# A four-layer network in three stages: 24 tile buffers of the second stage handed out by one plan

## The chip, the cores and the metric

The kernel runs on one core of a Trainium2 chip. The metric is the device time of one execution in microseconds (us). The times shown are medians of the runs; a profile is of one further execution, whose own time stands beside its span. Five engines work side by side, each in the order of its own queue: PE (TensorE, matmuls), DVE (VectorE), ACT (ScalarE), POOL (GpSimd) and SP (SyncE, which here only issues transfers). They wait for each other through semaphores.

## The reference

The input x is 8192 samples of 8 x 16 x 16 numbers in float32. Four layers follow, each a normalisation over groups of channels, a transformation, and a sum with its input:

```python
    # _gn: mean and variance over each of 4 groups of 2 channels, per sample
    # layer 0: three small tensor factors ("tensor train") and a bias
    x = x + _L0_conv_ref(_gn(x), L0_conv_core0, L0_conv_core1, L0_conv_core2, L0_conv_bias)
    # layer 1: 3x3 convolution, batch normalisation over all samples, gamma, beta, relu
    x = x + _L1_conv_ref(_gn(x), L1_conv_lin_w, L1_conv_lin_b, L1_conv_gamma, L1_conv_beta)
    # layer 2: 3x3 convolution of x quantised to -127..127 by the largest |x| of ALL samples
    x = x + _L2_conv_ref(_gn(x), L2_conv_weight, L2_conv_bias)
    # layer 3: 3x3 convolution with binarised weights, edge padding
    x = x + _L3_conv_ref(_gn(x), L3_conv_weight, L3_conv_bias)
```

Two of the steps need all samples before any can go on: the batch normalisation of layer 1 (its mean and variance) and the largest absolute value in layer 2. They cut the kernel into three stages.

## The kernel before, in words

The 8192 samples are 64 tiles (`NT = 64`) of 128 samples; one tile is 128 partitions x 2048 float32, 1 MB (`F = 2048`). A tile does not stay on the core from stage to stage: it is written to memory and read again, except where a buffer is kept for it.

**First stage.** For each tile layer 0 and the convolution of layer 1. It leaves two tensors a tile: `x1_d[t]` (x after layer 0) and `y_d[t]` (the convolution's result, not yet normalised). The last four tiles (`STAY = 4`) are not written: their x stands in the four `xs` buffers, their y in `ys` and `bs` (`y_stay`). The first stage also uses `xls`, two 1 MB buffers into which the split halves ("limbs") of a normalised tile are fetched; they are read by the matmuls of `expand`, and no more after the last of these.

**Between.** A small pool `bn` is opened after the first stage's pools are closed. In it the batch normalisation becomes a scale `bn_a` and a shift `bn_b` (lines 713 to 725). It is closed, and the pool `more` is opened with two tile buffers `xk`.

**Second stage** (from line 743). It takes the tiles in `order2`: the four that stayed first, then the others. For tile i:

- `relu2` (ACT) makes relu(bn_a y + bn_b) in place; `add2` (POOL) and `addv2` (DVE) add it to x, in the shares of the table `SPLIT`;
- `square2` (ACT) and `sums2` (64 matmuls) make the sums for the next normalisation, `stats2` (DVE reduction), `means2` (ACT), `sigma2` (DVE) and `power2` (POOL) turn them into mean and 1/sigma, `wide2` and `spread2` lay these out in PSUM;
- `centre2` subtracts the mean from x (DVE, a share `POOL2` of some tiles on POOL);
- `range2` takes maxima of the absolute value over w, `top2` (once for four tiles) scales and reduces them: these give the largest |x| of all;
- `store2` writes the centred x to `x2_d`, except for 15 tiles (`KEEP`) whose buffers are kept for the third stage.

Each of these steps has a time in a made-up clock of 6 units a tile: `when(op, i) = 6 i + PHASE2[op] + SHIFT2[...]`, the last for the final tiles only. All steps of all tiles, loads and stores too, are sorted by these times and written out in that order. The times thus fix only the order in each engine's queue, not when anything runs. SP's queue holds all loads and stores of this stage, so a transfer whose buffer is not free, or whose tile is not yet centred, holds those behind it.

The buffers before: x uses a ring of 15 (`x_slots`: the four `xs`, two `ex`, the halves of the two `us`, two `xk`, `ys`, `ys`, `bs`), y a ring of 8 (`y_slots`: `bs`, two `sq`, `xh`, four `yk`). x of tile i is loaded some 8 tiles before its use, y some 7; the last six tiles (`LATE = 6`) get theirs through `late2`, one load after each addition, into buffers of y that are just free. Tiles 43 to 57 are the 15 kept ones; 0 to 42 and 58 to 63 are stored. Nine loads (into `ex`, `us`, `sq`, `xh`) are written in the first stage's last steps. Two buffers (tag `sq2`) hold the squares.

**Third stage** (from line 908). It quantises by the largest |x|, and runs layers 2 and 3, first on the kept tiles, then on the others, which `load3` reads back into the same 15 buffers. Its first instruction on a tile is the DVE product `v`.

Nearly all engine instructions pass through one helper, so that they carry its line 43 in the profile; transfers carry the line of their own: 125 `load2`, 867 `late2`, 848 `store2`, 927 `load3`.

Of the kernel before, what the change touches and what calls it, by code (L numbers as in the profile page):

```python
# [8 lines left out]
F32 = mybir.dt.float32  # L9
F32R = mybir.dt.float32r  # L10
# [8 lines left out]
P = 128  # L19
C, H, W = 8, 16, 16  # L20
CH = C * H
F = P * W
G = 4
R = 8
NQ = 4
# [4 lines left out]
KEEP = 15  # L30


class InOrder:
# [5 lines left out]
    def __getattr__(self, name):  # L39
        op = getattr(self.engine, name)  # L40

        def call(*args, **kwargs):
# [13 lines left out]
TURN = 6.0  # L56
PHASE2 = {"relu": 0.0, "add": 0.3, "sums": 12.6, "rows": 18.9, "spr": 19.2, "sq": 7.5, "red": 13.8, "cp": 14.1, "cen": 20.4,
          "store": 20.7, "sig": 15.0, "pow": 15.3, "rng": 21.6, "top": 21.9, "addv": 0.31}
SHIFT2 = {-5: {"top": 9.4, "relu": -3, "sq": -1.3},
          -4: {"top": 18.3, "rng": 10.2, "cen": 1.4, "store": 11.7},  # L60
          -3: {"store": 4.0, "sums": -0.3, "cen": 3, "top": 33.8, "rng": 6.4, "sq": -4.0},
          -2: {"sums": -3.7, "spr": 1.0, "store": 8.4, "relu": -8.6, "rng": 12.1, "sq": -3.0, "top": 46.0, "red": -2.6},
          -1: {"cp": 0.1, "addv": 2.0, "red": 0.3, "pow": 1.3, "top": 60.5, "rng": 58.5, "store": 39.9, "spr": 10.6,
            "cen": 16.3, "relu": -4.3, "sq": -1.0}}

SPLIT = {0: 0.5, 1: 0.5, 2: 0.5, 3: 0.5, -2: 0.25, -1: 0.75, -3: 0.25}
POOL2 = {-4: 0.5, -3: 0.5, -2: 0.5, -1: 0.5, -5: 0.25}
SHARE = 24
# [8 lines left out]
def tile_net(ctx: ExitStack, tc: tile.TileContext, xb, xt_in, pack0, pack1, pack2, out):  # L77
    nc = tc.nc
    NT = xt_in.shape[0]
# [5 lines left out]
    x1_d = [dram.tile([P, F], F32, name=f"x1_d{t}", tag=f"x1_d{t}") for t in range(NT)]  # L85
    y_d = [dram.tile([P, F], F32, name=f"y_d{t}", tag=f"y_d{t}") for t in range(NT)]
    limb_d = [dram.tile([2, QS, 4 * BANK], F32, name=f"limb_d{k}", tag=f"limb_d{k}") for k in range(4)]
    x2_d = [dram.tile([P, F], F32, name=f"x2_d{t}", tag=f"x2_d{t}") for t in range(NT)]
# [13 lines left out]
    us = [hold.tile([P, 2 * F], F32, name=f"u{k}") for k in range(2)]  # L102

    STAY = 4
    order2 = list(range(NT - STAY, NT)) + list(range(NT - STAY))
    y_stay = [ys[NT % 2], ys[(NT - 1) % 2], bs[NT % 2], bs[(NT - 1) % 2]]
    y_of = dict(zip(order2, y_stay))

    x_slots = ([xs[t % 4] for t in order2[:STAY]] + ex + [u[:, h * F:(h + 1) * F] for u in us for h in range(2)] + y_stay[:3])
    y_slots = [y_stay[3]] + sqs + [xh]  # L110
    T2 = [dict() for _ in range(NT)]

    LATE = 6 if NT >= KEEP + STAY + 3 else 0
    stays = order2[max(0, NT - KEEP - LATE):NT - LATE]
    order = [*stays, *(t for t in range(NT) if t not in stays)]
    place = {t: i for i, t in enumerate(order)}

    def load2(i, what="yx"):
        for k in what:
            if k == "x":  # L120
                T2[i]["x"] = x_slots[i % KEEP]
            else:
                T2[i]["y"] = y_stay[i] if i < STAY else y_slots[(i - STAY + 1) % len(y_slots)]
            if i >= STAY:
                nc.sync.dma_start(T2[i][k], (x1_d if k == "x" else y_d)[order2[i]])


    first = ExitStack()
    const1 = first.enter_context(tc.tile_pool(name="const1", bufs=1))
    w0 = load_pack(pack0, PACK0, const1.tile(list(pack0.shape), F32, name="w0"))  # L130
# [211 lines left out]
    with first as s:  # L342
# [5 lines left out]

        T = [dict() for _ in range(NT)]

# [8 lines left out]

        xls = [const1.tile([P, F], F32R, name=f"xl{k}") for k in range(2)]  # L360

# [255 lines left out]
        for n in range(NT * NQ):  # L617
# [57 lines left out]
            if quarter_of(n, LAG):  # L675
                conv1(*quarter_of(n, LAG))
            for i, k in {NT * NQ - 6: [(0, "x"), (1, "x")], NT * NQ - 2: [(0, "y"), (2, "x"), (1, "y"), (3, "x")]}.get(n, []):
                load2(STAY + i, k)

        t = NT - 1  # L680
        seen = max(1, NT - 2)
        shift, nmean, part, last = bnw[:, 0:1], bnw[:, 1:2], bnw[:, 2:4], bnw[:, 4:6]
        dve.tensor_reduce(shift, bnst[:, 0:seen, 0], AX.X, ALU.add)
        load2(STAY + 4, "x")
        load2(STAY + 5, "x")
        conv1_output(t - 1, 1)
# [3 lines left out]
        quarter_apply(t, 2)  # L690
        load2(STAY + 2, "y")
        conv1_direct(t, 1)
# [49 lines left out]

    more = ctx.enter_context(tc.tile_pool(name="more", bufs=1))
    small = ctx.enter_context(tc.tile_pool(name="small", bufs=4))
    kept = {}
    with tc.tile_pool(name="p2", bufs=2) as p2, tc.tile_pool(name="ps2", bufs=2, space=PSUM) as ps2:
        T = T2
        x_slots[STAY + 6:STAY + 6] = [more.tile([P, F], F32, name=f"xk{k}") for k in range(2)]
        y_slots += [p2.tile([P, F], F32, name=f"yk{k}", bufs=1) for k in range(4)]
        psc = ps2.tile([P, 96], F32, name="psc2", tag="psc2", bufs=1)  # L750
# [39 lines left out]
        def square2(i):  # L790
            T[i]["sq"] = p2.tile([P, F], F32, name=f"sq2_{i}", tag="sq2")
            act.activation(T[i]["sq"], T[i]["x"], AF.Square)
# [51 lines left out]
        def store2(i):  # L844
            if NT - KEEP - LATE <= i < NT - LATE:
                kept[order2[i]] = T[i]["x"]
            else:
                nc.sync.dma_start(x2_d[order2[i]], T[i]["x"])

# [13 lines left out]

        def late2(n):
            k, j = "yx"[n % 2], NT - LATE + n // 2
            T2[j][k] = T[NT - LATE - AHEAD2 - 1 + n]["y"]
            nc.sync.dma_start(T2[j][k], (x1_d if k == "x" else y_d)[order2[j]])

        def when(op, i, more=0.0):
            return TURN * i + PHASE2[op] + SHIFT2.get(i - NT, {}).get(op, 0) + more  # L870

        AHEAD2, TURNX = len(y_slots) - 1, KEEP - 3
        for i in range(STAY):
            load2(i)
        for i, k in [(3, "y"), (6, "x"), (4, "y"), (7, "x"), (5, "y"), (6, "y")]:
            load2(STAY + i, k)
        OPS2 = {"relu": relu2, "add": add2, "addv": addv2, "sums": sums2, "rows": wide2, "spr": spread2, "sq": square2,
                "red": stats2, "cp": means2, "cen": centre2, "store": store2, "sig": sigma2, "pow": power2, "rng": range2,
                "top": top2}
        todo2 = [(when(op, i), OPS2[op], (i,)) for i in range(NT) for op in OPS2]  # L880
        todo2 += [(when("relu", i - AHEAD2, -.2), load2, (i, "y")) for i in range(STAY + AHEAD2, NT - LATE)]
        todo2 += [(when("add", i - TURNX, .6) if i < KEEP else when("relu", i - 8, -.1), load2, (i, "x"))
                  for i in range(TURNX, NT - LATE)]
        todo2 += [(when("add", NT - LATE - AHEAD2 - 1 + n, .6), late2, (n,)) for n in range(2 * LATE)]
        todo2.append((when("relu", NT // 2, -.3), operands3, ()))
        for _, f, args in sorted(todo2, key=lambda e: e[0]):
# [21 lines left out]
    with ExitStack() as s:  # L908
# [3 lines left out]
        T, T3 = [dict() for _ in range(NT)], {}  # L912
        AHEAD = min(NT, KEEP - 8)
        diag3 = diagonal("d")
# [6 lines left out]
        def load3(i):  # L921
            t = order[i]
            if t in kept:
                T[i]["x"] = kept[t]
                return
            T[i]["x"] = x_slots[(NT - KEEP - LATE + i) % KEEP]
            nc.sync.dma_start(T[i]["x"], x2_d[t])

# [243 lines left out]
```

## Time and profile before

| | us |
|---|---|
| median of 3 runs | 3795.26 (3795.01 to 3795.76) |
| the profiled execution: its time | 3795.71 |
| its span, first to last instruction | 3793.9 |
| second stage begins: first relu | 2625.94 |
| second stage ends: last maximum over a tile's values (starts 3046.16, takes 0.28) | 3046.44 |
| third stage begins: first `v` on DVE | 3051.20 |

The chain that ended last runs 79% on PE, 10% on DVE and 7% over transfers. Whole-span shares are averages over three different stages: PE is busy 94% of the span, DVE 87%, POOL 79%, ACT 67%; in the second stage PE is busy only half the time (13.74 of 20 us in the window from 2640), while the 16 transfer engines are full. The transfer queue of SP moves 688.03 MB in the whole kernel. A row of the timeline reads: start in us, duration, engine, line, operation, what is written and read (buffer numbers left out, so `yk` is any of the four), the shapes, how many, and in brackets the idle time before and what ended it. A row of SyncE gives the issue of a transfer, not its length.

### The profile page before, as it was taken

How to read it: one execution, taken by the hardware profiler on the slowest of the kernel's cores; microseconds unless marked ns; L12 is line 12 of the kernel's file. 1: busy time of each engine (PE TensorE's matmuls, PEld its weight loads, DVE VectorE, ACT ScalarE, POOL GpSimd, SP SyncE). 2: the span in 40 equal slices, each digit the busy share in tenths (PEclk: the TensorE clock that was granted, in tenths of full speed). 3: DMA queues.
4: the chain of work that ended last, by engine and by line, in shares of the span. 5: the costliest groups of instructions: out<-in, count | busy, mean ns of one | idle time of the engine just before them, and what ended most of it. 6: DMA issues, size and time to landing. Idle time of an engine off the chain costs nothing.

```text
span 3793.9 us, 63755 instructions
## 1 busy us (share of the span) xinstructions
PE 3568.5 (94%) x21896; PEld 2295.5 (61%) x21960; DVE 3317.6 (87%) x5963; ACT 2543.2 (67%) x2807; POOL 2990.9 (79%) x3102
## 2 busy tenths in 40 slices
PE   8999999999999999999999999998655569999999
PEld 4666666666666666666666666665544446666666
DVE  8888888888888888888888888887987888889887
ACT  5666666666666666666666666665765668888886
POOL 4877777777777778778777777775987869999998
PEclk9999999999999999999999999998776889999999
DMA  6787887887887887878878878865999824444432
GB/s 225 258 272 253 260 269 255 261 269 253 262 269 255 260 266 252 268 258 256 270 253 261 272 250 264 270 205 228 424 425 426 333 101 189 189 189 189 190 133 112
DMA packets 210276, 957.45 MB, mean 252 GB/s; under 512 B 44832, under 2 KB 45088, under 8 KB 109984
## 3 DMA queue, kind: packets, MB, share of 16 engines
q1 hardware_dynamic: 173232, 688.03, 48.7%
q0 software_dynamic: 36288, 264.26, 23.5%
q8 instruction: 175, 2.87, 0.3%
q14 instruction: 149, 1.22, 0.1%
q10 hardware_dynamic: 432, 1.08, 0.1%
HBM read 576.75 MB, written 376.44 MB: 251 GB/s over the span
## 4 chain that ended last, share of the span: by engine, by line
PE 79%; DVE 10%; DMA 7%; POOL 2%; issue 1%; ACT 1%; SPq 0%; DVEq 0%; POOLq 0%; ACTq 0%
PE po L43 45%; PE pu L43 12%; PE pf L43 6%; PE pm L43 6%; DVE v L43 3%; PE pc L43 3%; PE pq L43 3%; PE s L43 2%; DMA sq<-y_d 2%; DMA x_d<-u 1%; DMA ys<-x_d 1%; PE ps_a L43 1%; DVE top L43 1%; DVE xs L43 1%; DVE ys L43 1%
## 5 line engine op out<-in xcount | busy, mean ns | idle before, releaser
L43 PE MATMUL po<-u,core 128*128 128x512 f32 (+1 forms) x4112 | 1844.6, 591 | 0.6 <-DVE xs L43 0.6
L43 ACT COPY u<-pu 128x2048 f32<-128x2048 f32 x512 | 956.5, 1868 | 515.9 <-PE pu L43 515.9
L43 PEld LDWEIGHTS po<-u,core 128*128 128x128 f32 x4112 | 744.9, 190 | 737.4 <-issue 735.4
L43 PE MATMUL pu<-core2r,xl 128*128 128x256 f32 x4032 | 678.5, 310 | 4.8 <-ACT u L43 3.5
L43 PEld LDWEIGHTS pu<-core2r,xl 128*128 128x128 f32 x4032 | 527.9, 189 | 128.1 <-issue 123.1
L43 POOL TENSOR_TENSOR bs<-bs,xh 128x512 fp32r<-128x512 f32 (+1 forms) x253 | 325.8, 1288 | 202.1 <-ACT xh L43 202.1
L43 POOL TENSOR_TENSOR v<-e 128x128 f32<-128x128 f32 x750 | 397.3, 541 | 0.0
L43 DVE TENSOR_TENSOR xs<-po,xs 128x512 f32<-128x512 f32 x256 | 176.9, 691 | 220.2 <-PE po L43 220.2
L43 ACT ACTIVATE m<-pm,b 128x128 f32<-128x128 f32 x250 | 92.0, 368 | 396.7 <-PE pm L43 396.7
L43 PEld LDWEIGHTS pm<-v,fast 128*128 128x128 f32 x2000 | 262.5, 191 | 119.7 <-issue 106.4
L43 POOL TENSOR_TENSOR e<-x1n,x 128x512 f32<-128x512 f32 x250 | 306.0, 1224 | 26.4 <-ACT x L43 19.3
L43 DVE TENSOR_TENSOR bs<-bs,stat 128x1024 f32<-128x1024 f32 x252 | 290.5, 1214 | 2.1
L43 POOL TENSOR_TENSOR xs<-xs,w 128x2048 f32<-128x2048 f32 x64 | 291.5, 4555 | 0.6 <-DMA xs<-in_xt 0.6
L43 PE MATMUL pm<-v,fast 128*128 128x128 f32 x2000 | 263.5, 275 | 0.0
L43 ACT ACTIVATE x<-x1n 128x512 f32<-128x512 f32 x500 | 247.0, 545 | 7.6 <-DVE x1n L43 7.6
L43 PE MATMUL pf<-hi,sign 128*128 128x512 f32 x768 | 229.2, 434 | 0.0
L43 POOL DMA_DIRECT2D xl<-limb_d x252 | 150.0, 595 | 94.8 <-ACT x L43 33.8
L43 PE MATMUL pf<-lo,sign 128*128 128x512 f32 x768 | 217.6, 419 | 2.7 <-ACT lo L43 2.7
L43 POOL TENSOR_TENSOR v<-r 128x128 f32<-128x128 f32 x500 | 215.5, 447 | 0.0
L43 POOL TENSOR_TENSOR mvb<-mvb,mhalf 128x4 f32<-128x4 f32 x64 | 66.3, 1036 | 162.7 <-DVE mvb L43 142.7
L43 PE MATMUL pq<-q,band 128*128 128x480 bf16 (+1 forms) x704 | 186.7, 385 | 7.7 <-ACT q L43 4.1
L43 PE MATMUL gb<-ident,wide 128*128 128x128 f32 x128 | 42.3, 424 | 157.4 <-ACT wide L43 156.4
(337 smaller groups left out, 7303.3 us busy)
## 6 DMA issues: line engine op xcount, KB each, us to landing
xl<-limb_d POOLq DMA_DIRECT2D x252, 1024.0 KB, 7.4
x_d<-xs SPq DMA_DIRECT2D x72, 1024.0 KB, 8.4
xs<-in_xt SPq DMA_DIRECT2D x64, 1024.0 KB, 7.6
bs<-in_xb SPq DMA_DIRECT2D x63, 1024.0 KB, 5.8
limb_d<-xh SPq DMA_DIRECT2D x1008, 64.0 KB, 4.2
limb_d<-bs SPq DMA_DIRECT2D x1008, 64.0 KB, 5.2
y_d<-ys SPq DMA_DIRECT2D x60, 1024.0 KB, 8.1
yk<-y_d SPq DMA_DIRECT2D x30, 1024.0 KB, 19.6
```

Source lines behind the costliest of these rows:

```text
L43: return self.tc.keep_in_program_order(op(*args, **kwargs))
```

## The change

- `plan2` takes the place of the two rings and of `late2`. It walks through all wanted loads in order of time (a y is wanted 8.22 tiles before its relu, an x 7.54 tiles before its addition: `AHEAD2`) and gives each the buffer of one common set of 24 that its table of free times has free first. A buffer of y is taken to be free half a tile (`FREE2`) after its addition, one of x 0.8 tiles after its store. `BEGIN2` holds when the 16 loose buffers first come free.
- The stores of tiles 0 to 40 are written at 5.39 tiles behind the tile's start (`BEHIND2`), where before they came at 20.7 units, 3.45 tiles. Of the last 23 tiles 15 are kept; eight (`LATE = 8`) are stored as soon as they are centred, and the plan picks which: 51, 52, 56 and 58 to 62. Kept are 41 to 50, 53, 54, 55, 57 and 63.
- The buffers: one `sq2` fewer, one `yk` more (five). The two `xk` of the pool `more` now lie where the `xls` lay, since these have got a pool of their own, `limbs1`, opened ahead of all others of the first stage. The plan's first loads after `xh` go to these two.
- The nine loads in the first stage fill the same nine buffers, with y and x of tiles 4 to 7 and y of tile 8.
- New tables `SHIFT2`, `SPLIT` and `POOL2` for the last tiles: among others the addition of tile 62 is wholly DVE's, of 57 a quarter, of 60 and 63 a half; of the centring POOL does a half for tiles 59, 60 and 63, a quarter for 57, 61 and 62.
- The third stage takes its buffers from the plan (`x3`).

```diff
-SPLIT = {0: 0.5, 1: 0.5, 2: 0.5, 3: 0.5, -2: 0.25, -1: 0.75, -3: 0.25}
-POOL2 = {-4: 0.5, -3: 0.5, -2: 0.5, -1: 0.5, -5: 0.25}
+SPLIT = {0: 0.5, 1: 0.5, 2: 0.5, 3: 0.5, -2: 1, -1: 0.5, -7: 0.25, -4: 0.5}
+POOL2 = {-4: 0.5, -3: 0.25, -2: 0.25, -1: 0.5, -7: 0.25, -5: 0.5}
+AHEAD2 = {"y": 8.22, "x": 7.54}
+BEHIND2, LATE = 5.39, 8
+FREE2 = {"y": 0.5, "x": 0.8}
+BEGIN2 = {"ex0": -83.5, "ex1": -83, "sq0": -82.5, "sq1": -52, "u0": -30, "u1": -29.3, "u2": -21.8, "u3": -21.4,
+          "xh": -16.3, "xl0": -16.2, "xl1": -16.1, "yk0": -1.5, "yk1": -1.5, "yk2": -1.5, "yk3": -1.5, "yk4": -1.5}
...
+    LOOSE = {"y_3", "sq0", "sq1", "xh", *(f"yk{k}" for k in range(5))}
+    def plan2():
+        centred = [when("cen", i) + .05 for i in range(NT)]
+        stores = {i: max(centred[i], TURN * (i + BEHIND2)) for i in range(NT - KEEP - LATE)}
+        free = [(t, n) for n, t in BEGIN2.items()]
...
+        for want, k, i in wanted:
+            k, now = "yx"[k], max(want, last)
+            free.sort()
+            pick = free[0]
+            if k == "x" and i not in stores:
+                firm = [e for e in free if e[1] not in LOOSE]
+                if late < LATE and (not firm or firm[0][0] > now and pick[0] < firm[0][0]):
+                    late, stores[i] = late + 1, centred[i]
+                else:
+                    pick = firm[0]
+            elif k == "y" and i > NT - KEEP - LATE - 8:
+                pick = ([e for e in free if e[1].startswith("yk") and e[0] <= now] + [pick])[0]
+            free.remove(pick)
+            last = max(now, pick[0] + .05, last + .001)
+            T2[i][k] = pick[1]
+            loads.append((last, i, k))
...
     first = ExitStack()
+    limbs1 = first.enter_context(tc.tile_pool(name="limbs1", bufs=1))
     const1 = first.enter_context(tc.tile_pool(name="const1", bufs=1))
...
-        xls = [const1.tile([P, F], F32R, name=f"xl{k}") for k in range(2)]
+        xls = [limbs1.tile([P, F], F32R, name=f"xl{k}") for k in range(2)]
...
-            for i, k in {NT * NQ - 6: [(0, "x"), (1, "x")], NT * NQ - 2: [(0, "y"), (2, "x"), (1, "y"), (3, "x")]}.get(n, []):
-                load2(STAY + i, k)
+            early2(*{NT * NQ - 6: ("ex0", "ex1", "sq0"), NT * NQ - 2: ("sq1", "u0", "u1")}.get(n, ()))
...
     more = ctx.enter_context(tc.tile_pool(name="more", bufs=1))
+    tiles.update({f"xl{k}": more.tile([P, F], F32, name=f"xk{k}") for k in range(2)})
...
-        x_slots[STAY + 6:STAY + 6] = [more.tile([P, F], F32, name=f"xk{k}") for k in range(2)]
-        y_slots += [p2.tile([P, F], F32, name=f"yk{k}", bufs=1) for k in range(4)]
+        tiles.update({f"yk{k}": p2.tile([P, F], F32, name=f"yk{k}", bufs=1) for k in range(5)})
...
-            T[i]["sq"] = p2.tile([P, F], F32, name=f"sq2_{i}", tag="sq2")
+            T[i]["sq"] = p2.tile([P, F], F32, name=f"sq2_{i}", tag="sq2", bufs=1)
...
-        todo2 += [(when("relu", i - AHEAD2, -.2), load2, (i, "y")) for i in range(STAY + AHEAD2, NT - LATE)]
-        todo2 += [(when("add", i - TURNX, .6) if i < KEEP else when("relu", i - 8, -.1), load2, (i, "x"))
-                  for i in range(TURNX, NT - LATE)]
-        todo2 += [(when("add", NT - LATE - AHEAD2 - 1 + n, .6), late2, (n,)) for n in range(2 * LATE)]
+        todo2 += [(at, load2, (i, k)) for at, i, k in loads2] + [(at, store2, (i,)) for i, at in stores2.items()]
```

## The prediction

> Tiles are numbered 0 to 63 in the order of the second stage; y53 and x53 are the two 1 MB loads of tile 53, S53 its store.
>
> **What bounds the kernel now.** First the page's 40 slices: 27 to 32, counted from 0, are the second stage, the only part that the change touches.
>
> ```profile
> DMA  6787887887887887878878878865999824444432
> ```
>
> Slices 28 to 30 stand at 9: this stage is bound by transfers, the rest by TensorE. Then the windows by 20 us (span, PE, PEld, DVE, ACT, POOL busy, clock, DMA share, GB/s):
>
> ```profile
> 2620.00:2640.00 20.00, 10.43 (x142) 7.80 (x140) 9.98 (x23) 12.76 (x10) 11.74 (x6) 0.66 0.79 322
> 2640.00:2660.00 20.00, 13.74 (x272) 11.16 (x272) 19.52 (x28) 17.07 (x20) 19.25 (x7) 0.83 1.01 406
> ...
> 2980.00:3000.00 20.00, 12.27 (x269) 9.92 (x272) 19.01 (x28) 15.74 (x20) 20.00 (x8) 0.91 0.96 394
> 3000.00:3020.00 20.00, 9.73 (x184) 8.10 (x179) 19.88 (x21) 14.51 (x14) 15.70 (x7) 0.81 0.62 236
> ```
>
> Transfers are full (shares 1.01) from 2640 to 2980 and, at 0.79 of the window in which they start, from about 2625 on; from 2980 on DVE (19 to 20 of 20) and POOL are full, and DMA has room. Third, SyncE's issues in time:
>
> ```profile
> 2609.36 0.32 SPq L125 DMA_DIRECT2D xh<-y_d  x1
> 2623.02 0.32 SPq L125 DMA_DIRECT2D yk<-y_d  x1
> 2625.68 0.32 SPq L125 DMA_DIRECT2D xk<-x_d  x1
> ...
> 2973.76 0.32 SPq L867 DMA_DIRECT2D xh<-y_d  x1
> 2979.28 0.32 SPq L867 DMA_DIRECT2D yk<-x_d  x1
> ...
> 3012.80 0.32 SPq L867 DMA_DIRECT2D yk<-x_d  x1
> 3015.63 0.32 SPq L848 DMA_DIRECT2D x_d<-bs  x1
> 3023.55 0.32 SPq L848 DMA_DIRECT2D x_d<-sq  x1
> ```
>
> At 2973.76 y60 goes out, the last load of the full queue; it lands 19.6 us later by the DMA view, at 2993.4. The seven behind it go one by one as adds free buffers, to x63 at 3012.80, which lands in 4.7. The stores S58 and S59 follow. Last, the engines' timeline:
>
> ```profile
> 2963.63 4.57 POOL L43 TENSOR_TENSOR u<-u,sq 128x2048 f32<-128x2048 f32 x1 [1.85 <-ACT sq L43]
> ...
> 3008.74 3.45 POOL L43 TENSOR_TENSOR yk<-yk,yk 128x1536 f32<-128x1536 f32 x1 [0.39 <-ACT yk L43]
> ...
> 3009.01 3.73 DVE L43 TENSOR_TENSOR yk<-yk,yk 128x512 f32<-128x512 f32 x1
> ...
> 3046.16 0.28 DVE L43 TENSOR_REDUCE amax<-top 128x1 f32<-128x128 f32 x1
> ```
>
> Add 53 is the last that waits for a transfer (y53 lands, its relu runs from 2961.46). The 3.73 of DVE beside POOL's 3.45 is used below. Add 63 starts at 3024.63, and the last maximum ends at 3046.44; all of the third stage hangs on that.
>
> **A transfer's price.** Before y60 stand 120 loads less 9 made before 2623 less the 7 late ones, so y60 is load 104; with the stores of tiles 0 to 42 it is transfer 147. (2993.4 - 2623.02 - 4.7) / 146 = 2.505 us each.
>
> **Part 1, the start.** The same nine buffers (ex, sq, u, xh) are filled in the first stage, with other tiles. The tenth load is now x8 into the first limb buffer. That was last read at about 2592, but the batch-norm pool opens and closes in between and takes the lowest free address, which is now this buffer's. The trace shows it for the old xk, which stood at that address: its load waited, after the yk load before it, for
>
> ```profile
> SPq L125 <- DVE bn_b L725: 2.5, 1, 2.5
> ```
>
> SyncE issues in order, so the five yk loads wait behind it: the queue starts at 2625.7 instead of 2623.0, +2.7. Bounds: x8 and y9 go right behind xh at 2609.4, which removes these 2.7 and two transfers, 2 x 2.505 = 5.0: -7.7 against +0; I take the wait, by the row.
>
> **Part 2, loads ahead, stores behind.** Old order: 13 transfers stand from y53 to y60 (counted in SyncE's rows), so y53 is number 134. New order from the plan's sums: 111 loads follow the first nine, 41 stores (tiles 0 to 40) stand 5.39 turns behind. From x53 on the plan has y54 x54 y55 x55 y56 x56 y57 y58 x57 x58 y59 S51 x59 y60 S52 x60 y61 y62 x61 x62 S56 y63 S58 S59 x63: 20 loads after x53, so x53 is number 91 + 41 = 132. It is now x53 that add 53 waits for, its relu being done: two transfers fewer, -5.0; the later start, +2.7; relu to add, 2963.63 - 2961.46 = 2.17, no longer in line. Add 53 starts 4.5 earlier, at 2959.1. This is the whole gain; the number of transfers hardly falls (y63 is 154 of 157).
>
> **Part 3, the last ten tiles.** Adds run on POOL 5.52 apart (2980.28, 2985.80, 2991.33 in the old trace). Four steps bring add 57 to 2981.2. A quarter of it now goes to DVE (SPLIT -7), which the 3.73 row prices: 512 elements cost some 0.6 (half of 1.21 for 1024) but last until POOL's add is over. DVE, full here, loses 3.1 at most, 0 at least; the reductions and powers behind it, and with them the next add, wait: I take 2.7, near the row. Add 58 starts at 2989.4, 59 at 2994.9, 60 (half and half) 6.7 later because both halves follow each other, at 3001.6. Then POOL centres a quarter of 57 (1.0), makes a power (1.0), waits for relu 61: add 61 at 3008.6, end 3013.2. Add 62 is DVE's alone: behind centre 58 (2.35), a small one (0.15), range 58 (2.33), reduction 60 (0.51) it starts at about 3016.0 and, at 2 x 1.21, ends at 3018.4. POOL's half of centre 59 (1.93 by the old rows) reads SBUF too and goes by the same row after it: 3020.4.
>
> Here lies the new wait. x63 takes y62's buffer, free at 3018.4; but S59 stands before it on SyncE and waits for centre 59. S59 goes at 3020.4, and x63 behind it lands 4.4 (what S58 took, alone) + 2.45 (the spacing of issues in the full queue) later, at 3027.3, ten us after the old one. Add 63 starts then, 2.7 later than before. From there DVE has, in the order of the new plan: half add 1.21, reduction 0.51, centre 60 1.21, 0.15, reduction 0.51, 1.8 until POOL's add and centre halves (2.3 + 1.9) are over, range 2.33, 0.15, centre 61 1.77, 0.3 for POOL, range 2.33, reduction 63 0.51, centre 62 1.77, 0.15, range 2.33, centre 63 1.21, maxima 1.38, range 2.33, maxima 0.58: 22.5. The last maximum ends at 3049.8 against 3046.4: **+3.4**.
>
> The Trainium skill, SBUF — State Buffer, "Who interferes with whom", says that DVE with two SBUF inputs and a GpSimd instruction that reads SBUF never overlap: the later one is held until the other is done. It speaks against splitting adds between these two and against giving add 62 to DVE just ahead of POOL's centring; the 3.73 row agrees, and without the rule that half would end some 2 us sooner and the sum be +1.4. The same page ("Summary: rules for kernel authors") would have HBM transfers reckoned at about 358 GB/s: 2.93 us each, 65 us more over 152 of them, in either kernel; the windows' 426 GB/s go against that.
>
> **Costed at nothing.** One square buffer for two: a square waits for the previous sums, which end 1.5 us before it (squares on ACT start 2975.04 and 2980.66, the sums between end 2979.14); without that slack it costs up to 1 us a tile, 9 over the last nine. SHIFT2 changes the order alone; the list above is in the new one. S60 to S62 go after x63 beside DVE's list; uncovered, a store costs 4.4. The third stage keeps 15 tiles and reloads 49 as before: the first reload goes at 3100.99, long after.
>
> **Sum.** 3795.71 in the profiled execution (3793.9 span and 1.8 around it) + 3.4 = 3799.1; the median of the runs, 3795.26, lies 0.45 lower: **3798.7**. That is +0.09%, inside the 0.2% (7.6 us) that a measurement of this kernel can tell from none.
>
> **Rivals.** *The gain reaches the end, faster.* If the limb buffers are free of the batch-norm wait (-7.7) and x63 goes ahead of S59 (3018.4 + 0.1 + 4.7 = 3023.2, not 3027.3: -4.1): 3798.7 - 11.8 = 3786.9. For it: the limbs are done at 2592, and SyncE's order is not always the program's (the two ex loads, written near the first stage's end, go at 69.81 and 122.53). Against: the bn_b wait, and from 2623 on the old issues follow the written order throughout. One of the two alone gives 3791 to 3794.6: no change.
>
> *The late stores hold SyncE, slower.* Place: S59 ahead of x63. The old S59 waited 7.5 us on SyncE until 3023.55, harmlessly, since no load stood behind it. If the lead of 4.5 is lost in the split adds, and whole add 62 (2.43 for 0.61) is added, S59 goes at 3023.55 + 1.8 = 3025.4, 5.0 later than reckoned: 3803.7. It decides from an S59 at 3024.6 on. For it: DVE has no room from 2980 on. Against: add 53 does start earlier, and POOL runs without gaps.
>
> *The change doesn't do what it says*: putting stores off moves no transfer out of the queue. That is part of the forecast.
>
> **How the numbers follow.** Forecast 0.58, faster rival 0.20, slower 0.22. The forecast's own range: -2.7 (no loss at add 57) and -2.0 (no shared port) below, +4.1 (up to the slower rival's point) above: 3794 to 3803. For 8 in 10 it reaches over both rivals' prices: 3785 to 3808. Faster 0.20, same 0.58, slower 0.22.
>
> **What would show it.** Right: first load of the new queue at 2625.7, not 2609; add 53 at about 2959; no load between y63 and x63 for some 10 us, S59 issued just ahead of x63; last maximum near 3050; third stage as long as before (742.7 from its first v at 3051.20). Wrong: limb buffers filled at 2610, x63 out before 3015, DMA share under 1 before 2990 (then the put-off stores starve the queue, and all landings above are late), or squares waiting for PE.

## The result

| | before | changed |
|---|---|---|
| median of the runs, us | 3795.14 (3793.68 to 3795.76, 4 runs) | 3817.36 (3814.07 to 3820.00, 4 runs) |
| ratio | | 1.0059 (95%: 1.0041 to 1.0076) |
| profiled execution: time, span | 3795.71, 3793.9 | 3820.00, 3818.2 |
| first relu (end of stage one) | 2625.94 | 2636.92 |
| first relu to the end of the last maximum (stage two) | 420.50 | 430.69 |
| last maximum to first `v` | 4.76 | 5.33 |
| first `v` to the end (stage three) | 742.74 | 745.28 |

The changed kernel is 22 us slower, by 0.59%; forecast were 3.4 us, with a range up to 3808. The four rows split the 24.3 us of the two profiled spans: 11.0 in stage one, 10.2 in stage two, 0.6 between, 2.5 in stage three. The prediction had 3.4 for stage two and nothing for the others.

**Stage one.** The groups of instructions by line (busy us, mean ns of one, then idle time before), first of the kernel before:

```profile
L43 PE MATMUL po<-u,core 128*128 128x512 f32 (+1 forms) x4112 | 1844.6, 591 | 0.6 <-DVE xs L43 0.6
L43 PE MATMUL pu<-core2r,xl 128*128 128x256 f32 x4032 | 678.5, 310 | 4.8 <-ACT u L43 3.5 <-DMA xl<-limb_d 1.3
```

and of the changed one:

```profile
L43 PE MATMUL po<-u,core 128*128 128x512 f32 (+1 forms) x4112 | 1845.1, 592 | 0.0
L43 PE MATMUL pu<-core2r,xl 128*128 128x256 f32 x4032 | 689.6, 313 | 4.7 <-ACT u L43 3.6 <-DMA xl<-limb_d 0.8 <-ACT m L43 0.2
```

One group is 11.1 us busier, with the same number of instructions and the same waits: the matmuls of `expand`, whose weights are read from the limb buffers `xl` and whose moved operand is the constant `core2r`. Each takes 2.7 ns longer in the mean, though not all alike: in a group of eight that are issued together, the distance from one start to the next grows from 118 to 125 ns and from 115 to 123 at two places, and at the others changes by 4 ns or less. TensorE bounds this stage, so all of it reaches the end: the shift of these matmuls against the old kernel grows evenly, some 0.18 us a tile.

**Stage two.** The windows by 20 us of the changed kernel (span, PE, PEld, DVE, ACT, POOL busy, clock, DMA share, GB/s). Its stage lies 10.98 later, so 2980 here is 2969 there:

```profile
2980.00:3000.00 20.00, 12.65 (x208) 10.41 (x208) 19.84 (x25) 13.89 (x16) 16.22 (x7) 0.67 0.96 380
3000.00:3020.00 20.00, 11.22 (x203) 8.98 (x203) 17.34 (x25) 12.82 (x17) 15.12 (x7) 0.76 0.91 326
3020.00:3040.00 20.00, 11.24 (x176) 8.80 (x179) 14.31 (x14) 10.31 (x13) 10.42 (x4) 0.63 0.69 253
```

Before, POOL had 20.0 and 15.7 and DVE 19.0 and 19.9 in the two windows from 2980; now, from 3000 on, both stand idle for part of each window. Something is late for them. SyncE's issues show what:

```profile
2634.22 0.32 SPq L162 DMA_DIRECT2D yk<-x_d  x1
2636.66 0.32 SPq L162 DMA_DIRECT2D xk<-x_d  x1
...
2977.92 0.32 SPq L883 DMA_DIRECT2D x_d<-xh  x1
2980.37 0.32 SPq L162 DMA_DIRECT2D sq<-x_d  x1
2998.85 0.32 SPq L162 DMA_DIRECT2D xh<-y_d  x1
2999.26 0.38 SPq L883 DMA_DIRECT2D x_d<-bs  x1
2999.73 0.38 SPq L162 DMA_DIRECT2D sq<-x_d  x1
3010.03 0.32 SPq L162 DMA_DIRECT2D bs<-y_d  x1
3010.44 0.38 SPq L162 DMA_DIRECT2D xk<-y_d  x1
3010.93 1.16 SPq L162 DMA_DIRECT2D yk<-x_d  x2
...
3036.04 0.32 SPq L883 DMA_DIRECT2D x_d<-sq  x1
3036.45 0.38 SPq L162 DMA_DIRECT2D xk<-x_d  x1
```

(The first two rows belong to the start of the stage and are used further below.) At 2977.92 the store of tile 51 goes out of `xh`, and the next load but one, y60, goes into `xh`. It stands 18.5 us, with all behind it, and goes at 2998.85. The store of tile 52 (from `bs`) follows at once, and y61, which goes into `bs`, stands another 10.3. Then come y62 and, at 3010.93, x61 and x62. At the end, store 59 (3036.04) and right behind it x63. The DMA view (median us from issue to landing, 2975 to 3012) says why the waits are that long:

```profile
x_d<-xh SPq DMA_DIRECT2D x1, 1024.0 KB, 20.8
xh<-y_d SPq DMA_DIRECT2D x1, 1024.0 KB, 8.6
x_d<-bs SPq DMA_DIRECT2D x1, 1024.0 KB, 10.7
bs<-y_d SPq DMA_DIRECT2D x1, 1024.0 KB, 7.2
```

A store issued into the full queue frees its buffer 20.8 us later. SyncE's own waits over the whole kernel (us in total, times, the longest) name stores as what ended them; the longest of the second row is y61's, of the third y60's:

```profile
SPq L162 <- DMA x_d<-u: 59.5, 8, 12.1
SPq L162 <- DMA x_d<-bs: 25.7, 4, 9.8
SPq L162 <- DMA x_d<-xh: 24.0, 2, 18.0
```

Waits of this kind are common in the changed kernel: with the rows for the other buffers, 41 loads of the stage wait for a store to land, 262 us in all. Most cost nothing. The longest of the first row is x53's, which takes the buffer of store 39: SyncE issues nothing from 2945.84 to 2958.37, and yet transfers go on landing 2.4 to 2.6 us apart, since three others stand between this store and x53 and keep the queue filled. Between store 51 and y60 there is one, x59. It lands at 3001.12 and y60 at 3007.45, 6.3 us later: here the queue runs short. What POOL makes of it (its timeline, in brackets the idle time and what ended it):

```profile
2968.30 4.55 POOL L43 TENSOR_TENSOR u<-u,yk 128x2048 f32<-128x2048 f32 x1 [1.95 <-DMA u<-x_d]
...
2997.62 1.02 POOL L43 TENSOR_TENSOR gnst<-gnst,mhalf 128x4 f32<-128x4 f32 x1 [3.39 <-DVE gnst L43]
...
3024.87 4.50 POOL L43 TENSOR_TENSOR yk<-yk,bs 128x2048 f32<-128x2048 f32 x1 [7.01 <-DMA yk<-x_d]
3029.32 3.07 POOL L43 TENSOR_TENSOR gnst<-gnst,mhalf 128x4 f32<-128x4 f32 x1
3034.07 1.94 POOL L43 TENSOR_TENSOR sq<-sq,gm 128x1024 f32<-128x1024 f32 x1 [1.68 <-ACT gm L43]
...
3044.38 3.39 POOL L43 TENSOR_TENSOR xk<-xk,yk 128x1024 f32<-128x1024 f32 x1 [7.41 <-DMA xk<-x_d]
```

The first row is add 53, the fourth from the end add 61: POOL stands 7.0 us for x61. Behind add 61, on the same engine, comes the power of tile 59; without it there is no centre 59 (3034.07), without that no store 59, and behind store 59 stands x63, for which POOL waits 7.4 us before add 63. So one late load goes through two head-of-line waits (waits in which everything behind stands too) to the last tile. The last maximum (DVE's timeline):

```profile
3067.32 0.29 DVE L43 TENSOR_REDUCE amax<-top 128x1 f32<-128x128 f32 x1
```

### The profile page after: what moved, and what is told of

The parts are those of the page before. It is cut to its first block, busy times and chain, and to the rows that moved or that the text cites. A ratio compares the mean times of both kernels' runs of the same rounds, so it can differ in the third digit from the quotient of the medians.

```text
span 3818.2 us, 63818 instructions
## 1 busy us (share of the span) xinstructions
PE 3586.0 (94%) x21960; PEld 2306.9 (60%) x21960; DVE 3324.3 (87%) x5965; ACT 2545.6 (67%) x2808; POOL 2988.6 (78%) x3102
## 4 chain that ended last, share of the span: by engine, by line
PE 78%; DVE 9%; DMA 6%; POOL 4%; issue 1%; ACT 1%; SPq 0%; DVEq 0%; POOLq 0%; ACTq 0%
PE po L43 44%; PE pu L43 13%; PE pm L43 6%; PE pf L43 5%; DVE v L43 3%; PE pc L43 3%; PE pq L43 3%; PE s L43 2%; DMA x_d<-bs 1%; DMA x_d<-yk 1%; DVE xs L43 1%; POOL gnst L43 1%; DMA x_d<-xs 1%; PE ps_a L43 1%; DVE u L43 1%
## 5 line engine op out<-in xcount | busy, mean ns | idle before, releaser
L43 PE MATMUL pu<-core2r,xl 128*128 128x256 f32 x4032 | 689.6, 313 | 4.7 <-ACT u L43 3.6
L43 PEld LDWEIGHTS pu<-core2r,xl 128*128 128x128 f32 x4032 | 536.4, 189 | 128.4 <-issue 123.3
L43 POOL TENSOR_TENSOR bs<-bs,xh 128x512 fp32r<-128x512 f32 x252 | 320.9, 1274 | 211.1 <-ACT xh L43 211.1
```

The source lines that it names most:

```text
L43: return self.tc.keep_in_program_order(op(*args, **kwargs))
```

## The experiments

All kernels are compared with the one before, whose median in five sets of runs was 3794.8, 3795.2, 3794.7, 3794.8 and 3794.0. "Stage two" is first relu to last maximum of the profiled execution. One caution for that row: six kernels with the changed kernel's own second stage gave 430.7, 431.4, 426.9, 426.7, 429.4 and 427.0, so single profiles of it differ by up to 4.7, and a smaller difference of two rows says little.

### Stage one: where the limb buffers lie

**1. The kernel before, with the pool of the limb buffers alone.**

```diff
+    limbs1 = first.enter_context(tc.tile_pool(name="limbs1", bufs=1))
     const1 = first.enter_context(tc.tile_pool(name="const1", bufs=1))
-        xls = [const1.tile([P, F], F32R, name=f"xl{k}") for k in range(2)]
+        xls = [limbs1.tile([P, F], F32R, name=f"xl{k}") for k in range(2)]
```

> The kernel before, with one edit: the two limb buffers come from a pool of their own, opened first, so that they lie 24 KB lower and the other tiles of the first stage's pool 16 KB higher; the second stage is the old one. Theory A (the limb buffers' place makes the 4032 matmuls of `expand` 2.7 ns longer each): their mean is 312 to 313 ns for 310, the first relu starts at 2636.9 for 2625.9, the time is 3795.1 + 11 = 3806. Rival B (the first stage is slowed by something in the new second stage: other early loads, other code): 310 ns, first relu at 2625.9, time 3795.

Measured: 3805.84 (7 runs), ratio 1.0029 (1.0017 to 1.0040), first relu at 2637.70, stage two 421.7. The group of the matmuls:

```profile
L43 PE MATMUL pu<-core2r,xl 128*128 128x256 f32 x4032 | 689.5, 313 | 5.4 <-ACT u L43 3.3 <-DMA xl<-limb_d 2.0
```

The whole of stage one's loss, from these two lines alone. Theory A holds, B falls.

**2. The changed kernel, with these two lines undone.**

> The changed kernel, with the pool of the limb buffers taken back: they lie in the first stage's pool as before; the second stage is the new one. Theory A: first relu at 2626, matmuls of `expand` at 310 ns, time 3817.4 - 11 = 3806.4, and what is left, some +11 against before, is the second stage's. Rival B: first relu at 2637, 3817.

Measured: 3807.55, 1.0033 (1.0020 to 1.0046), first relu at 2625.61, 310 ns, stage two 431.4. As theory A has it; what is left, 12.7 us over the old kernel, is from stage two on.

**3. The limb buffers in the new place, shifted by 832 bytes; 4. core2r shifted by 192, the limb buffers not.**

```diff
     limbs1 = first.enter_context(tc.tile_pool(name="limbs1", bufs=1))
+    pads = [limbs1.tile([P, 208], F32, name="pad0")]        (run 3)
...
+        pads.append(const1.tile([P, 48], F32, name="pad1"))   (run 3)
+        pads = [const1.tile([P, 48], F32, name="pad1")]       (run 4)
         xls = [limbs1.tile([P, F], F32R, name=f"xl{k}") for k in range(2)]
```

> The changed kernel, with 832 bytes ahead of the limb buffers and 192 after the normalised tiles: the limb buffers stay in their new place, but stand to a multiple of 1024 bytes as they did before (and so do the weights' partner, the moved matrix core2r). Theory A1 (what counts is the address within 1024 bytes): first relu at 2626, 310 ns. A2 (what counts is the region): 2637, 313 ns.

> The changed kernel, with 192 bytes ahead of the moved matrix core2r: the limb buffers keep their new place (a multiple of 1024 bytes), core2r now stands to them, within 1024 bytes, as it did before (32 behind). Theory A1a (the limb buffers' own address within 1024 bytes counts): still 313 ns, first relu near 2637. A1b (how the two operands of the matmul stand to each other counts): 310 ns, first relu near 2626.

Measured: run 3 3805.83 (7 runs), first relu 2625.00, 310 ns; run 4 3802.92 (one run), first relu 2625.46. Run 4's group:

```profile
L43 PE MATMUL pu<-core2r,xl 128*128 128x256 f32 x4032 | 678.6, 310 | 4.7 <-ACT u L43 3.4 <-DMA xl<-limb_d 1.2
```

In run 4 the limb buffers lie exactly where the slow kernel has them, and moving the other operand by 192 bytes brings the old speed back. The reverse is given too: by the sizes of the tiles in the pools, core2r lies at the same place in the kernel before and in run 1, the one fast and the other slow. So A1b: it isn't the place of either tile, but how the two stand to each other. The pad of run 4 moves all tiles that lie behind it, not core2r alone; that core2r is the one that counts, the moved operand of the slower matmuls, is argued and not shown.

**5 and 6. core2r shifted by 64 and by 32 bytes** (the same pad, 16 and 8 numbers).

> The changed kernel with core2r moved by 64 bytes: it now stands to the limb buffers 928 behind within 1024, which is 32 within 128. If only the distance within 128 bytes counts, the matmuls of `expand` take 310 ns and the first relu comes at 2626; if a longer stretch counts, 313 and 2637.

> The changed kernel with core2r moved by 32 bytes: 896 behind the limb buffers within 1024, 0 within 128, and core2r itself now at a multiple of 64 bytes. If a distance of 96 within 128 was the slow one: 310 ns, 2626. If nearness of the two (896 to 1024) is: 313 ns, 2637.

Measured: 3812.46 and 3807.70, first relu at 2631.83 (312 ns) and 2628.45 (311 ns), one run each. The groups of run 5 and run 6:

```profile
L43 PE MATMUL pu<-core2r,xl 128*128 128x256 f32 x4032 | 685.4, 312 | 4.9 <-ACT u L43 3.5 <-DMA xl<-limb_d 1.5
L43 PE MATMUL pu<-core2r,xl 128*128 128x256 f32 x4032 | 682.2, 311 | 4.8 <-ACT u L43 3.6 <-DMA xl<-limb_d 1.3
```

Neither expectation fits: both are between the fast and the slow one. By the sizes of the tiles that lie between, core2r starts 16,416 bytes behind the first limb buffer in the kernel before, 40,800 in the changed one, 40,992 in runs 3 and 4, 40,864 and 40,832 in runs 5 and 6. Against multiples of a limb buffer's 8192 that is 32 past, 160 short, 32 past, 96 short and 128 short, with the group busy 0, 11.1, 0, 6.9 and 3.7 us longer than before (the first relu, which differs by up to 2 us among the kernels with 310 ns, comes 11.0, 5.9 and 2.5 later in the three slow ones). The loss is graded, and not in the order of the distance: 128 short costs less than 96. That the distance decides is shown, with this reserve; by what rule is open, and so is whether 8192 is the length that counts, since the two fast distances agree in every smaller power of two as well (only up to 128 is ruled out, by run 5).

### Stage two: loads behind stores

**7. The load of x63 ahead of store 59**, in the changed kernel; **8. the same with the limb buffers back.**

```diff
-    todo2 += [(at, load2, (i, k)) for at, i, k in loads2] + ...
+    todo2 += [(when("addv", 62) + .01 if (i, k) == (63, "x") else at, load2, (i, k)) for at, i, k in loads2] + ...
```

> The changed kernel, with the load of x63 written right behind the addition of tile 62, ahead of the store of tile 59. Theory C (that store, waiting for centre 59, holds x63 back): x63 goes out 4 to 5 us earlier, add 63 starts 4 to 5 earlier, and the last maximum comes 3 to 5 earlier: 3812 to 3814.5. Rival D (DVE's list after add 62 is what ends last, or the transfers before x63): x63 is earlier, the last maximum moves by under 1 us, 3816.5 to 3817.5.

> The changed kernel with the limb buffers back in their old place and the load of x63 ahead of the store of tile 59: the two earlier edits together. If they add up, 3807.5 - 6.6 = 3801; if the second one's gain was chance in part, 3803 to 3805.

Measured: run 7 3810.73 (4 runs), 6.6 below the changed kernel; x63 goes out 392.9 after the first relu for 399.5, add 63 starts at 399.1 for 407.5, stage two 422.4. Theory C holds. The gain is more than the 3 to 5 expected, and the edit does not explain all of it in the profile, where add 61, ahead of it, is 1.7 us earlier as well. The rows of x63 and add 63:

```profile
3029.24 0.32 SPq L162 DMA_DIRECT2D xk<-x_d  x1
3035.49 2.39 POOL L43 TENSOR_TENSOR xk<-xk,yk 128x1024 f32<-128x1024 f32 x1 [0.82 <-ACT yk L43]
```

Run 8: 3799.80 (10 runs), 1.0012 (1.0002 to 1.0021), stage two 422.7: the two edits add up.

**9 and 10. Other buffers for the last loads, first form**, with the limb buffers back; run 10 also has x63 in its buffer early:

```diff
     loads2, stores2 = plan2()
+    other = {"y60": ("sq1", 331.3), "y61": ("xh", 338.0), "x60": ("yk2", 343.0), "y62": ("y_3", 345.0),
+             "x61": ("yk4", 349.0), "x62": ("yk3", 355.0), "y63": ("yk0", 357.0)}   (run 10: "x63": ("xl0", 358.0) too)
+    for j, (at, i, k) in enumerate(loads2):
+        if f"{k}{i}" in other:
+            T2[i][k], at = other[f"{k}{i}"]
+            loads2[j] = (at, i, k)
+    loads2.sort()
```

> The changed kernel with the limb buffers back, and the last loads given other buffers: y60 goes into the buffer of y55, free after add 55, instead of that of x51, free when store 51 has landed; y61 takes x51's, x60 y57's, y62 x52's, x61 y58's, x62 y59's, y63 x56's. x63 stays behind store 59. Theory E (SyncE stands 18.5 us with y60 until store 51 has landed and 10.3 us with y61 until store 52 has, so that x61 comes 5 us late): y60 goes out right after x59, no gap of over 8 us in SyncE's issues before tile 63's x, add 61 starts 4 to 6 us earlier, the stage ends 3 to 6 earlier than with the limbs back alone: 3801.5 to 3804.5. Rival F (the loads of y60 and y61 come early enough, and POOL and DVE set the time of add 61): add 61 moves by under 1, time 3806.5 to 3808.

> As the kernel before it in this list (limbs back, other buffers for the last loads), and x63 goes out behind y63, ahead of store 59, since its buffer is free after add 56. Theories C and E: both costs gone, SyncE never holds a load behind a store of the last eight for over 8 us, stage 2 near 418 to 421 us, time 3793 to 3798. Rival: the tail is DVE's, whatever the loads do: not under the better of the two single edits, 3800 or more.

Measured: 3806.77 and 3808.45, stage two 431.9 and 434.7: no gain. y60 does go out 3.5 us behind x59, but DVE's timeline shows a new wait of my own making:

```profile
3015.29 2.35 DVE L43 TENSOR_REDUCE top<-yk 128x64 f32<-128x1024 f32 x2 [17.36 <-DMA yk<-y_d]
```

y63 was written at 357.0, ahead of the maxima of tile 56 (357.6), whose buffer it takes. The maxima had to wait for the load, and are taken over y63 there in place of x56. Both expectations (3801.5 to 3804.5 and 3793 to 3798) were missed. These two runs say nothing on theory E; they say that an order by planned times has to keep every reader of a buffer ahead of its next load.

**11 and 12. The same with y63 behind those maxima** (358.0, and x63 at 359.0).

> The kernel of the other buffers for y60 to y63 again (limbs back, x63 still behind store 59), with the load of y63 moved behind the maxima of tile 56: in the earlier form it stood ahead of them, although it takes that tile's buffer, so that DVE waited 17.4 us for its landing. Theory E: y60 right behind x59, x61 some 3 to 5 us earlier than with the limbs back alone, add 61 too; store 59 and x63 follow 2 to 5 earlier: stage 2 at 426 to 429 for 431.4, time 3802.5 to 3805.5. Rival F (x61 and add 61 were not what set the end): 431, 3807.

> As the kernel before it, and x63 (whose buffer is free after add 56) written behind y63, ahead of store 59. Theories C and E: against the kernel with the limbs back and x63 ahead alone (3799.8, stage 2 at 422.7) add 61 starts 3 to 5 us earlier and the last maximum 3 to 5 earlier: stage 2 at 418 to 420, time 3795 to 3797. Rival (the tail is DVE's list after add 60 or 62, whatever lands): 422 to 423, 3799 to 3800.

Measured: run 11 3797.28 (10 runs), 1.0007 (0.9998 to 1.0017), stage two 421.0; run 12 3793.39 (10 runs), 0.9996 (0.9986 to 1.0005), stage two 418.6. Run 11 differs from run 2 only in the buffers and places of seven loads, and is 10.3 us faster, more than the 2 to 5 expected; which of the seven bring how much was not separated. SyncE's issues of run 12 (its stage one ends at 2625.0):

```profile
2968.66 0.32 SPq L169 DMA_DIRECT2D sq<-x_d  x1
2972.20 0.32 SPq L169 DMA_DIRECT2D sq<-y_d  x1
2973.61 0.32 SPq L889 DMA_DIRECT2D x_d<-bs  x1
2987.42 0.32 SPq L169 DMA_DIRECT2D xh<-y_d  x1
2987.84 0.37 SPq L169 DMA_DIRECT2D yk<-x_d  x1
```

y60 follows x59 after 3.5 us for 18.5, and store 52 after another 1.4. y61, now in the buffer of tile 51, still stands 13.8, but behind a queue that is full for longer than that (store 52 lands 21.1 us after its issue by the DMA view). Add 61 starts 380.1 after the first relu, in both runs, for 387.9 in the changed kernel. Theory E holds, and is the larger part of stage two's loss. The two costs overlap: from run 2 on, x63 ahead alone is worth 7.8 us (run 8), the other buffers alone 10.3 (run 11), both 14.2 (run 12).

**13. The stores of tiles 0 to 40 not put off** (in the kernel of run 8).

```diff
-    ... [(at, store2, (i,)) for i, at in stores2.items()]
+    ... [(when("cen", i) + .05 if i < 41 else at, store2, (i,)) for i, at in stores2.items()]
```

> Limbs back and x63 ahead (3799.8), and the stores of tiles 0 to 40 written where the tile is centred, 2 tiles earlier than the plan puts them: the putting off alone is undone. Theory G (the putting off itself moves no transfer out of the full queue ahead of x53; the lead of 6 us at add 53 comes from two more tiles stored late): add 53 within 1.5 us, time within 2 of 3799.8. Rival H (the putting off lets loads pass stores that are not ready): add 53 5 to 7 later, time 3804 to 3808.

Measured: 3804.14 (10 runs), 1.0024 (1.0015 to 1.0034); add 53 starts 337.9 after the first relu for 332.0 in run 8, and 337.7 in the old kernel. I had expected no change (theory G); H, that the put-off lets loads pass stores that are not ready, holds. The windows, of run 8:

```profile
2620.00:2660.00 40.00, 22.87 (x414) 17.78 (x412) 29.25 (x50) 29.97 (x29) 31.46 (x12) 0.79 0.90 363
```

and of this run:

```profile
2620.00:2660.00 40.00, 22.75 (x413) 17.65 (x411) 29.34 (x50) 29.98 (x29) 31.61 (x13) 0.79 0.79 308
```

A DMA share of 0.79 for 0.90 over 40 us is 4.4 us of idle transfer engines: between these two rows SyncE issues nothing,

```profile
2627.04 0.76 SPq L162 DMA_DIRECT2D yk<-y_d  x1
2643.19 0.32 SPq L882 DMA_DIRECT2D x_d<-xs  x1
```

because the first store waits for its tile to be centred and the loads stand behind it. From 2660 to 2940 both are at 1.01 or 1.02. So at the stage's start the place of a store decides whether the queue gets full. The 4.4 are most of the 5.9 us that add 53 loses; the rest was not traced.

**14. Add 57 wholly on POOL** (in the kernel of run 8: `-7: 0.25` taken out of `SPLIT`).

> Limbs back and x63 ahead (3799.8), and the addition of tile 57 wholly on POOL (no quarter on DVE). The prediction's step (the split costs POOL 2.7 us, by the shared port): add 58 starts 2 to 3 us earlier. If the loads of tiles 60 to 62 set add 61, the gain is lost there: stage 2 within 1 of 422.7, 3799 to 3800.5. Rival (POOL and DVE set the end): 2 to 3 less, 3797 to 3798.

Measured: 3797.13 (10 runs, 3793.70 to 3802.01) for 3799.80 (3796.50 to 3807.45), but stage two of the profiled executions 425.2 for 422.7. Add 58 starts 359.3 after the first relu for 362.4, and add 60 at 376.5 for 375.8: in these profiles the gain is gone by add 60, which waits for x60. Median and profile disagree, the latter by less than single profiles differ; left unclear here.

**15 to 18. Towards the best version.** Run 15 is run 12 with x60 written ahead of y61 (y61 at 343.5); run 16 the same with add 57 whole; runs 17 and 18 are these two with y63 in the buffer of y60 (`"y63": ("sq1", 360.4)`), so that it no longer waits for store 56.

> The kernel with the other buffers and x63 ahead (3793.4), and x60 written ahead of y61, which stands 14 us waiting for store 51: x60's buffer is free at the end of add 57, some 4.5 us before. If y61's wait is what makes add 60 late there (it waits 1.5 us for x60), add 60 starts 1 to 1.5 earlier, the time is 3791 to 3793; if POOL's order sets it, 3793 to 3794.

> As the kernel before it, and the addition of tile 57 wholly on POOL. With the loads of 60 to 62 in time, the 2.3 us that the split costs POOL at add 58 should reach the end: 3789 to 3791. If DVE's list behind add 60 sets the end, as before: 3791 to 3793.

> The kernel with x60 first (add 57 split), and y63 in the buffer of y60, free after add 60 (at about 3002), in place of that of x56, which waits for store 56 to land (3010.9): the last load behind a late store. If that wait is the last of its kind on the way to the end, relu 63 no longer waits, add 63 starts some 2 us earlier and the time is 3790.5 to 3792; if DVE's list sets the end, 3793.

> As the kernel before it, and the addition of tile 57 wholly on POOL: relu 63 no longer waits the 2.1 us that it does in the kernel with add 57 whole, the time is 3790 to 3792, below the old kernel by 3 to 5; if DVE's list sets the end, 3793.5.

| run | median, us | ratio (95%) | stage two |
|---|---|---|---|
| 15 | 3793.12 (11 runs) | 0.9996 (0.9987 to 1.0005) | 418.5 |
| 16, add 57 whole | 3793.61 (11) | 0.9996 (0.9987 to 1.0005) | 417.8 |
| 17 | 3791.44 (11) | 0.9992 (0.9983 to 1.0001) | 415.6 |
| 18, add 57 whole | 3791.04 (11) | 0.9991 (0.9982 to 1.0000) | 416.4 |

The split of add 57 makes no difference that can be told (15 against 16, 17 against 18). Run 16 misses both its expectations (3789 to 3791, 3791 to 3793). Runs 17 and 18 are 1.7 and 2.6 us below 15 and 16, where some 2 were expected of the last load behind a late store; but the old kernel was 0.8 lower in that set as well, and the intervals overlap. SyncE's issues of run 18, from y61 on:

```profile
2988.09 0.32 SPq L169 DMA_DIRECT2D xh<-y_d  x1
2995.62 0.32 SPq L169 DMA_DIRECT2D bs<-y_d  x1
2996.03 1.38 SPq L169 DMA_DIRECT2D yk<-x_d  x2
2997.50 0.69 SPq L889 DMA_DIRECT2D x_d<-yk  x1
2998.24 0.43 SPq L169 DMA_DIRECT2D xk<-x_d  x1
3001.57 0.32 SPq L169 DMA_DIRECT2D sq<-y_d  x1
3007.08 0.32 SPq L889 DMA_DIRECT2D x_d<-yk  x1
3017.58 0.32 SPq L889 DMA_DIRECT2D x_d<-sq  x1
```

All loads (the last is y63, 3001.57) are out before store 58, and stage two is some 4 us shorter than in the old kernel. With the plan's loads mended and the limb buffers back the new scheme is 2.5 to 2.9 us below the old kernel, at the edge of what the runs can tell.

## Why the prediction was wrong

It forecast 3798.7, which is 3799.1 for the profiled execution; that took 3820.0. Of the 20.9 us between, 11.0 lie in stage one, 6.8 in stage two and 3.1 behind. Two steps failed: a term that was put at nothing (the first stage), and the wait of loads for the buffers of stores just ahead of them (add 61).

**The first stage, wrong.** Its step is the sentence on the slices, "27 to 32 ... are the second stage, the only part that the change touches". The move of the limb buffers was followed only to the batch-norm wait; that the matmuls which read them are among the most numerous of a stage bound by TensorE was not weighed, and no bound was put on it. Runs 1 to 4 show the price, 2.7 ns in the mean on 4032 matmuls. A bound of 3 ns on each, a size known only from these runs, is 12 us; it would have brought the upper end from 3808 to 3820.

The Trainium skill, TensorE: Matmul & The Clock Gate, "Step-by-step: what each phase is for", says that PE has two independent SBUF read ports, one for the streamed operand and one for the weights, and that loading the next weights takes no read bandwidth from a running matmul. From that one would expect the places of the two operands to make no difference; in runs 1 to 6 they do: with the same instructions, a shift of 192 bytes takes 11 us off. Whether the weight load is what disturbs the matmul was not shown.

**The start, wrong, small.** +2.7 was reckoned for x8 waiting behind the batch norm, with the other loads behind it. x8 did wait (2636.66, less 10.98: 2625.68), but the load of x9 into a `yk` buffer, written behind it, went out at 2634.22 (2623.24): in SyncE's queue as built it stands ahead of x8. The queue starts as before: 0 for +2.7. The order of a queue is read from the built program or the trace, not from the source.

**Transfers ahead of add 53, right in size, the mechanism in part.** Two transfers fewer at 2.505 and relu no longer in line gave -7.2 without the late start; measured 2968.30 - 10.98 = 2957.3 against 2963.63, -6.3. Not foreseen: that the putting off is needed for it. The prediction gave it no worth of its own; without it add 53 is where the old kernel has it (run 13).

**The split of add 57, right.** Predicted was a loss of 2.7 on POOL. POOL stood 3.39 before the next power (2997.62), and add 58 starts 7.8 us after add 57 where whole adds lie 5.5 apart: a loss of 2.3. The power beside DVE's whole add 62 (4.24 us from 3027.28) took 3.07 us, where others take 1.0, and ended 0.9 after it; that fits the rule that the prediction used. With the loads mended the split makes no difference at the end that can be told (runs 15 to 18).

**Adds 58 and 59, right; add 60, right by luck; add 61, the step that failed.** In the changed kernel, less 10.98: add 58 2987.6 (predicted 2989.4), add 59 2993.1 (2994.9), add 60 3001.5 (3001.6), add 61 3013.9 (3008.6). Ahead of add 60 POOL stood 2.3 us until x60, held behind y60, had landed at 3012.34 (in run 7, where the order up to there is the same, the row of add 60 names x60's load as what ended the wait); that wait was not in the sum, and makes up for adds 58 and 59 being 1.8 early. The prediction wrote the transfers down in order, "y59 S51 x59 y60 S52 x60 y61 ...", and counted each at 2.505, as if SyncE went on issuing. It did not ask which buffer each load takes: y60 takes the one that S51 is just leaving, y61 that of S52. A store issued into the full queue lands some eight transfers, 20.8 us, later. The prediction had such a time in hand (y60 of the old kernel lands 19.6 us after its issue) and used it only for that load. Run 11 shows the price: 10.3 us in the median, 6.4 where x63 goes ahead already (run 12 against run 8).

**S59 ahead of x63, right in kind.** Predicted was S59 at 3020.4 and x63 landing at 3027.3; measured 3025.06, and add 63 at 3033.4. This is the slower rival's 3025.4, reached by another way: not a lead lost in split adds, but add 61 late, the power of 59 behind it, centre 59 behind that. Run 7: 6.6 us. The rest of the tail, 23.2 from add 63 to the last maximum, is near the 22.5 predicted. So of the 6.8 us that stage two lacks, S59 brings 4.7, the way from S59 to add 63 1.4 and the tail 0.7.

**Costed at nothing, in part right.** The single square buffer: no square waits for PE in the changed kernel. The first stage and the third stage were not at nothing. Stage three took 743.8 to 745.3 in nine kernels with the plan's own last loads, 741.8 to 743.0 in the others and before, save that of run 14 (742.6). The difference, up to 2.5 us, comes in steps of 0.35 at the same tiles. Its cause was not tried and stays open.

**The judgement of size.** The slower rival stood at 0.22 with 3803.7 as its price; mechanism and sign were in the text, but it was bounded by one place, S59, where there were three that cost (y60, y61, x63), and 0.58 went to their being harmless. Of its signs, x8 at 2625.7, add 53 and S59 just ahead of x63 came as written; between y63 and x63 lay 22.9 us for "some 10", and the last maximum came 6.8 late.

## What to carry to other kernels

When a plan hands a buffer from a store to a load, price the load from the store's landing, not from its issue: in a full queue that is all transfers in flight (here 20.8 us), and SyncE, which issues in order, holds every transfer behind that load. Then count the transfers written between the two: with three between them such a wait was harmless here, with one the queue ran short. When an edit moves a tile, look up every instruction that reads it, in stages that the edit seems to leave alone as well, and multiply a few ns by its count. An experiment that changes the place of one buffer alone costs two lines, and separates such a cost from the rest of a change.

## What was not expected of the hardware

- The same 4032 matmuls (weights 128 x 128, moved operand 128 x 256) took 310, 311, 312 or 313 ns in the mean with the distance between the two operands' addresses; no added wait appears in any row. The loss in busy time is 0 at 32 bytes past a multiple of 8192, and 6.9, 3.7 and 11.1 us at 96, 128 and 160 short of one. The rule is open.
- In single profiles of one and the same second stage its length differed by up to 4.7 us. In the three long ones (429.4 to 431.4) x61 landed 386.5 to 387.8 us after the first relu, in the three short ones (426.7 to 427.0) 383.4 to 383.9. Why was not found.
- A store of 1 MB that SyncE issued into the full queue landed 20.8 us later, while transfers landed 2.4 to 2.6 us apart; SyncE could issue nothing for 12.5 us, before a load that took the buffer of a store with three transfers between, and no landing was late.
